# Softmax scores sent through DRAM and used an iteration later, in a 64-graph residual network kernel

One core of one Trainium2 chip. The metric is device time in microseconds (us), the median of several executions. The program runs on one core, so a run has one span and one granted TensorE clock; every run told here is of the fast state, with a granted clock of 0.995 to 0.999 (0.996 to 0.998 in the profiled runs).

## The reference

Two graph layers, each followed by a residual and a layer norm, over 64 graphs of 256 nodes with 512 features, in float32.

```python
def _L0(x, adj, W):
    deg = jnp.sum(adj, axis=-1, keepdims=True)
    agg = jnp.einsum('bij,bjf->bif', adj, x) / jnp.maximum(deg, EPS)
    return jax.nn.relu(jnp.einsum('bnf,of->bno', jnp.concatenate([x, agg], axis=2), W))

def _L1(X, adj, mask, Wqk, Wv):
    q, k = jnp.split(X @ Wqk, 2, axis=-1)
    v = X @ Wv
    agg = jnp.einsum('bij,bjd->bid', adj, k * mask[:, :, None])
    w = inv_scale * mask * jnp.einsum('bid,bid->bi', q, agg)     # one score a node
    return jax.nn.softmax(w, axis=1)[:, :, None] * v             # over the graph's 256 nodes

x = _layernorm(x + _L0(x, adj, W))
x = _layernorm(x + _L1(x, adj, nodemask, Wqk, Wv))
```

## The kernel before

One loop goes over the graphs as a software pipeline: iteration i runs layer 0 of graph i, layer 1's products of graph i-2, and the softmax and last stage (`finish`) of an older one. All products are cut into 2x2 blocks and multiplied in a seven-product scheme, so TensorE adds into one open accumulator `u` again and again, and between two such products ScalarE must copy `u` out. Layer 0's first part:

```python
def layer0_a(g):
    ...
    product(u, s["A11"], w["B11"])
    began = nc.scalar.copy(own[:, 0, :], u)
    product(p5, s["S1"], w["T1"])
    product(u, s["S2"], w["T2"], start=False)
    nc.scalar.copy(y[:, 0, :], u)
    product(p2, s["A12"], w["B21"])
    nc.vector.tensor_add(own[:, 0, :], p2, own[:, 0, :])
    product(u, s["S3"], w["T3"], start=False)
    nc.scalar.copy(y[:, 1, :], u)              # must end before the next product into u
    ...
def layer0_b(g):
    product(u, s["A22"], w["T4"], start=False) # "t,xT" in the profile
```

The scores of a graph lie one to a partition, but the softmax runs over the nodes. The kernel turns the scores of two graphs at a time into rows by TensorE and the probabilities back:

```python
def softmax_rows(k):                           # two graphs, every other iteration
    ...
    for t in range(NT):
        nc.tensor.transpose(wr[:, t, :], w[:, t, :], ident)
    nc.vector.reduce_max(top, wr.rearrange("g t p -> g (t p)"), axis=AX.X)
    ...
    nc.scalar.activation(e, wr, AF.Exp, bias=top, accum_out=total)
    ...
def softmax_cols(k, e):
    for t in range(NT):
        nc.tensor.transpose(ps[:, t, :], e[:, t, :], ident[:G, :G])
    nc.vector.tensor_copy(probs[k], ps)
```

A scheduler puts each engine's instructions in order from the program's text. `with tc.issue_after(ins):` holds what is written in its block behind `ins`, on the engine of `ins` alone; it sets an order and adds no wait.

Of the kernel before, what the change touches and what calls it, by code (L numbers as in the profile page):

```python
# [31 lines left out]
F32 = mybir.dt.float32  # L35
AF = mybir.ActivationFunctionType
# [2 lines left out]

P = 128  # L40
Q = 32
G = 2
DEG_EPS = 1e-6
LN_EPS = 1e-5

# [2 lines left out]
def resnorm_kernel(  # L48
# [21 lines left out]
    const = ctx.enter_context(tc.tile_pool(name="const", bufs=1))  # L70
    pool = ctx.enter_context(tc.tile_pool(name="pool", bufs=2))
    small = ctx.enter_context(tc.tile_pool(name="small", bufs=4))
    ps_mm = ctx.enter_context(tc.tile_pool(name="ps_mm", bufs=7, space=bass.MemoryType.PSUM))
    ps_tp = ctx.enter_context(tc.tile_pool(name="ps_tp", bufs=1, space=bass.MemoryType.PSUM))

    (xs, adjs, rows, xTs, sums0, sumsA, rdegs, vals, owns, x1s, x1Ts, sums1, aggs, vs, scores, probs,
     open0) = ({} for _ in range(17))

    def first(out, in_):

# [20 lines left out]
    with setup as sp:  # L101
        wqk = sp.tile([P, 2 * NA, F], F32, name="wqk")
        for a in range(NA):
            src = wqk_t.rearrange("(h a p) f -> a p h f", p=P, h=2)[a]
            first(wqk.rearrange("p (h a) f -> a p h f", h=2)[a], src)
        w0_of = w_t.rearrange("(k h p) o -> k p h o", p=P, h=H)
        for k in (0, 2):
            first(w0[:, k * H:(k + 1) * H, :], w0_of[k])
        load_t(0, first)
        for k in (3, 1):  # L110
            first(w0[:, k * H:(k + 1) * H, :], w0_of[k])
        load(0, first)
        mask_sb = const.tile([P, NT, B], F32, name="mask_sb")
        first(mask_sb, mask_t)
        load_t(1, first)
        load(1, first)
        loaded = first(w1[:, NF:, :], wv.rearrange("(c p) o -> p c o", p=P))

        ident = const.tile([P, P], F32, name="ident")
        make_identity(nc, ident)  # L120
        eps = const.tile([P, 1], F32, name="eps")
        nc.vector.memset(eps, LN_EPS)

        ps = [ps_mm.tile([P, F], F32, name="mm") for _ in range(NF)]
        for a in range(NA):
            for c in range(NF):
                nc.tensor.matmul(ps[c], wqk[:, a, c * P:(c + 1) * P], wqk[:, NA + a, :],  # L127
                                 start=(a == 0), stop=(a == NA - 1))
        for c in range(NF):
            nc.scalar.copy(w1[:, c, :], ps[c])  # L130
# [28 lines left out]
    def bank():  # L159
        return ps_mm.tile([P, F], F32, name="mm")  # L160
# [44 lines left out]
    def layer0_a(g):  # L205
        s, w = sums0[g], W0
        own = owns[g] = pool.tile([P, NT, F], F32, name="own")
        y = values(g)[:, 0]
        u, p5, p2 = bank(), bank(), bank()
# [3 lines that stand above are left out]
        product(u, s["S2"], w["T2"], start=False)  # L213
        nc.scalar.copy(y[:, 0, :], u)
        product(p2, s["A12"], w["B21"])
        nc.vector.tensor_add(own[:, 0, :], p2, own[:, 0, :])
        product(u, s["S3"], w["T3"], start=False)
        nc.scalar.copy(y[:, 1, :], u)  # L218
        nc.vector.tensor_add(y[:, 1, :], p5, y[:, 1, :])
        open0[g] = u, p5  # L220
        return began

    def layer0_b(g):
        s, w, own, y = sums0.pop(g), W0, owns[g], values(g)[:, 0]
# [12 lines left out]
    def gather_a(g):  # L237
# [7 lines left out]
        nc.vector.tensor_sub(t1, b12, b11)  # L245
        nc.vector.tensor_sub(t2, b22, t1)
        nc.vector.tensor_sub(t3, b22, b12)
        nc.vector.tensor_sub(t4, b21, t2)
        w = {"B11": b11, "B21": b21, "B22": b22, "T1": t1, "T2": t2, "T3": t3, "T4": t4}
        zr = aggs[g] = pool.tile([P, 2, NT, F], F32, name="zr")  # L250
        r11, r12, r21, r22 = (zr[:, k0:k1, t, h * HF:(h + 1) * HF] for t in range(NT) for h in range(2))
# [9 lines left out]
        def steps():  # L261
# [17 lines left out]
            twice(p5, "S4", "B22", start=False)  # L279
            nc.vector.tensor_add(r12, of(p5), r12)  # L280
            yield
        return steps()

    def combine0(g):
        own, z, rdeg, xg = owns[g], aggs[g][:, 0], rdegs.pop(g), xs.pop(g)
# [4 lines left out]
                                           op0=OP.max, op1=OP.add)  # L290

    def norm0(g):
        x1s[g] = pool.tile([P, NT, F], F32, name="x1", bufs=G + 4)
        layer_norm(owns.pop(g), x1s[g])
        for t in range(NT):
            nc.scalar.activation(values(g + 1)[:, 1, t, :], x1s[g][:, t, :], AF.Copy,  # L296
                                 scale=mask_sb[:, t, g:g + 1])
        x1Ts[g] = pool.tile([P, NF, N], F32, name="x1T")
        transpose_rows(x1s[g], x1Ts[g])
# [2 lines left out]
        sums1[g] = row_sums(x1Ts.pop(g), nc.vector)  # L302

    def layer1_steps(g):
        if g % G == 0:
            scores[g // G] = (small.tile([P, NT, G], F32, name="scores", bufs=2),
                              small.tile([P, G], F32, name="part", bufs=2))
        sc, part = scores[g // G]
        at = g % G
        s, w, agg = sums1.pop(g), W1, aggs.pop(g + 1)[:, 1]  # L310
        v = vs[g] = late.tile([P, NT, F], F32, name="v", bufs=G + 2)
        q = pool.tile([P, F], F32, name="q")

        def dot(a, t, to):
            nc.vector.scalar_tensor_tensor(q, a, 1.0, agg[:, t, :], op0=OP.mult, op1=OP.mult, accum_out=to)  # L315

        u = bank()
        product(u, s["A11"], w["B11"])
        nc.scalar.copy(q, u)
        dot(q, 0, part[:, at:at + 1])  # L320
        yield
        p5 = bank()
        product(p5, s["S1"], w["T1"])
        yield
        product(u, s["S2"], w["T2"], start=False)
        nc.scalar.copy(v[:, 0, :], u)  # L326
        yield
        p2 = bank()
        product(p2, s["A12"], w["B21"])
        dot(p2, 0, sc[:, 0, at:at + 1])  # L330
        yield
        product(u, s["S3"], w["T3"], start=False)
        nc.scalar.copy(v[:, 1, :], u)  # L333
        nc.vector.tensor_add(v[:, 1, :], p5, v[:, 1, :])  # L334
        yield
        product(u, s["A22"], w["T4"], start=False)
        dot(u, 1, sc[:, 1, at:at + 1])
        yield
        product(p5, s["S4"], w["B22"], start=False)
        nc.vector.tensor_add(v[:, 0, :], p5, v[:, 0, :])  # L340
        yield

    def softmax_rows(k):
        w, part = scores.pop(k)
        nc.vector.tensor_add(w[:, 0, :], w[:, 0, :], part)
        nc.vector.scalar_tensor_tensor(w, w, inv_scale, mask_sb[:, :, k * G:(k + 1) * G],
                                       op0=OP.mult, op1=OP.mult)
        wr = ps_tp.tile([G, NT, P], F32, name="tp")
        for t in range(NT):
            nc.tensor.transpose(wr[:, t, :], w[:, t, :], ident)  # L350
        top = small.tile([G, 1], F32, name="top")
        nc.vector.reduce_max(top, wr.rearrange("g t p -> g (t p)"), axis=AX.X)
        nc.vector.tensor_scalar(top, top, -1.0, None, op0=OP.mult)
        e = small.tile([G, NT, P], F32, name="e", bufs=2)
        total = small.tile([G, 1], F32, name="total")
        nc.scalar.activation(e, wr, AF.Exp, bias=top, accum_out=total)
        nc.vector.reciprocal(total, total)
        nc.vector.tensor_scalar(e, e, total, None, op0=OP.mult)
        return e

    def softmax_cols(k, e):
        ps = ps_tp.tile([P, NT, G], F32, name="tp")
        for t in range(NT):
            nc.tensor.transpose(ps[:, t, :], e[:, t, :], ident[:G, :G])  # L364
        probs[k] = small.tile([P, NT, G], F32, name="probs", bufs=2)
        nc.vector.tensor_copy(probs[k], ps)

    def finish(g):
        x1, v, p = x1s.pop(g), vs.pop(g), probs[g // G]
        o = pool.tile([P, NT, F], F32, name="o")  # L370
        for t in range(NT):
            nc.vector.scalar_tensor_tensor(o[:, t, :], v[:, t, :], p[:, t, g % G:g % G + 1], x1[:, t, :],  # L372
                                           op0=OP.mult, op1=OP.add)
        layer_norm(o, o)
        nc.sync.dma_start(out[g].rearrange("(t p) f -> p t f", p=P), o)
# [3 lines left out]
    def step(gen, n=1):  # L379
        for _ in range(n):  # L380
            next(gen, None)

    for i in range(B + G + 2):
        new = i < B
        if i + 2 < B:
            with tc.issue_after(loaded.ins):
                loaded = load(i + 2)
        if i == 1:
            W1 = weight_sums(w1, "t1_")
        k, at = divmod(i - G - 2, G)  # L390
        e = None
        if new:
            began = layer0_a(i)
        if at == 0 and 0 <= k < B // G:
            e = softmax_rows(k)
        if 0 <= i - 2 < B:
            turn(i - 2)
        l1 = layer1_steps(i - 2) if 0 <= i - 2 < B else iter(())
        step(l1)
        if new:  # L400
            layer0_b(i)
        if e is not None:
            softmax_cols(k, e)
        if 0 <= i - 2 - G < B:
            finish(i - 2 - G)
        z = gather_a(i) if i <= B else iter(())
        step(l1, 2)
        step(z)
        step(l1)
        step(z)  # L410
        step(l1)
        step(z)
        step(l1)
        step(z)
        step(l1)
        step(z)
        if new:
            combine0(i)
            norm0(i)
        if i + 1 < B:  # L420
            with tc.issue_after(began.ins):
                prepare(i + 1)


# [24 lines left out]
```

## Time and profile before

| | before |
|---|---|
| median of three runs | 1999.58 us (1999.43 to 1999.61) |
| span of the profiled run | 1996.4 us |
| busy: TensorE, VectorE, ScalarE | 99%, 76%, 31% |
| an iteration with / without softmax transposes | 30.78 / 30.16 us |
| 59 iterations, from the start of i = 4 (120.49) to that of i = 63 (1918.55) | 1798.06 us |

A profile names an instruction by engine, source line and operation, with its output and inputs (`mm<-t,xT` is the product of the weights `t` with `xT` into an accumulator bank). PE is TensorE, DVE VectorE, ACT ScalarE, POOL GpSimd, and SPq the SP queue, in which SyncE issues the DMAs. A line of a timeline has the start and the duration in us, the engine, source line, operation, output and inputs, and in brackets the idle time before it and what ended it. Line numbers move by four between the kernels: L156 and L218 here are L160 and L222 after. A line of the waits has the waiter and the awaited: us in total, times, longest. `PEld` is TensorE's weight load.

### The profile page before, as it was taken

To read this page: it belongs to the slowest core of one execution; us is meant where nothing else is said; L and a number is where in the kernel's file an instruction comes from. 1 tells how busy PE (TensorE), PEld (TensorE's weight loads), DVE (VectorE), ACT (ScalarE), POOL (GpSimd) and SP (SyncE) were. 2 spreads that over 40 slices of the span, in tenths; PEclk is the share of its full clock that TensorE was granted. 3 is DMA by queue.
4 is the path that set the end of the run, shared out by engine and by line. 5 is a ranking of instruction groups with operands and counts; after the bars stand their busy time and mean duration, and the time that the engine had idled before them with its cause. 6 is when DMAs were issued, how large, how long until landed. Compare 5 with 4: busy or idle time off the path is not lost.

```text
span 1996.4 us, 19070 instructions
## 1 busy us (share of the span) xinstructions
PE 1968.4 (99%) x5536; PEld 1029.0 (52%) x5536; DVE 1514.0 (76%) x3056; ACT 628.1 (31%) x1417; POOL 411.1 (21%) x518
## 2 busy tenths in 40 slices
PE   8999999999999999999999999999999999999996
PEld 3555555555555555555555555555555555555552
DVE  5667778777787777787777877777877778777776
ACT  2323333233233233332332332333323323323321
POOL 3122122221221121222212212212222121122100
PEclk9999999999999999999999999999999999999998
DMA  6333332332333333323333333333233233333211
GB/s 222 85 79 77 97 90 73 91 93 79 92 75 94 92 77 97 90 74 91 92 81 91 75 95 93 75 96 90 75 90 93 80 91 76 95 94 74 74 43 53
DMA packets 384902, 174.38 MB, mean 87 GB/s; under 512 B 283808, under 2 KB 349472, under 8 KB 384800
## 3 DMA queue, kind: packets, MB, share of 16 engines
q1 hardware_dynamic: 384800, 173.17, 32.9%
q8 instruction: 46, 0.75, 0.2%
q14 instruction: 56, 0.46, 0.1%
HBM read 105.97 MB, written 33.55 MB: 70 GB/s over the span
## 4 chain that ended last, share of the span: by engine, by line
PE 96%; DVE 2%; SPq 1%; DMA 0%; ACT 0%; issue 0%; DVEq 0%; ACTq 0%
PE mm L156 76%; PE mm L255 19%; SPq L171 1%; PE mm L127 1%; PE tp L364 0%; PE tp L350 0%; DVE st L178 0%; DMA xT<-x_t 0%; DMA wqk<-wqk_t 0%; DVE own L289 0%; DVE own L287 0%; DVE o L372 0%; ACT vals L296 0%; DVE x L184 0%; DMA x1T<-sq 0%
## 5 line engine op out<-in xcount | busy, mean ns | idle before, releaser
L156 PE MATMUL mm<-w,s 128*128 128x512 f32 x1024 | 481.2, 592 | 0.0
L156 PE MATMUL mm<-t,s 128*128 128x512 f32 x1024 | 463.9, 595 | 0.0
L156 PEld LDWEIGHTS mm<-t,s 128*128 128x128 f32 x1024 | 192.1, 190 | 229.2 <-issue 213.6
L156 PEld LDWEIGHTS mm<-w,s 128*128 128x128 f32 x1024 | 194.6, 190 | 191.1 <-issue 162.6
L156 PE MATMUL mm<-w,x1T 128*128 128x512 f32 x512 | 240.8, 593 | 2.3 <-DMA x1T<-sq 2.3
L156 PE MATMUL mm<-w,xT 128*128 128x512 f32 x512 | 240.9, 592 | 0.0
L197 POOL TENSOR_TENSOR sa<-adj 128x128 f32<-128x128 f32 x64 | 45.8, 716 | 780.0 <-PE mm L255 778.5
L148 POOL TENSOR_TENSOR s<-xT 128x256 f32<-128x256 f32 x64 | 46.7, 730 | 704.5 <-PE mm L156 685.4
L255 PE MATMUL mm<-tv,sa 128*128 128x256 f32 x768 | 187.5, 379 | 0.4 <-DVE tv L245 0.4
L255 PEld LDWEIGHTS mm<-tv,sa 128*128 128x128 f32 x768 | 145.8, 190 | 76.1 <-issue 60.1
L229 DVE TENSOR_TENSOR vals<-mm,vals 128x512 f32<-128x512 f32 x64 | 44.3, 692 | 134.6 <-PE mm L156 134.6
L156 PEld LDWEIGHTS mm<-w,xT 128*128 128x128 f32 x512 | 97.3, 190 | 94.6 <-issue 91.3
L334 DVE TENSOR_TENSOR v<-mm,v 128x512 f32<-128x512 f32 x64 | 44.3, 692 | 130.9 <-ACT v L333 130.9
L287 DVE SCALAR_TENSOR_TENSOR own<-zr,rdeg,own 128x512 f32<-128x512 f32 x128 | 107.6, 841 | 42.4 <-ACT zr L277 42.3
L156 PEld LDWEIGHTS mm<-w,x1T 128*128 128x128 f32 x512 | 94.8, 190 | 83.7 <-issue 79.4
L315 DVE SCALAR_TENSOR_TENSOR q<-mm,zr 128x512 f32<-128x512 f32 x128 | 88.1, 688 | 65.6 <-PE mm L156 65.6
L326 ACT COPY v<-mm 128x512 f32<-128x512 f32 x64 | 37.4, 585 | 298.1 <-PE mm L156 298.1
L156 PE MATMUL mm<-t,x1T 128*128 128x512 f32 x256 | 125.5, 612 | 0.9 <-ACT v L333 0.7
L255 PE MATMUL mm<-vals,adj 128*128 128x256 f32 x512 | 121.6, 380 | 2.3 <-DVE vals L229 1.9
L156 PE MATMUL mm<-t,xT 128*128 128x512 f32 x256 | 120.6, 593 | 2.8 <-ACT vals L218 2.8
L255 PEld LDWEIGHTS mm<-vals,adj 128*128 128x128 f32 x512 | 97.0, 190 | 44.6 <-issue 25.1
L372 DVE SCALAR_TENSOR_TENSOR o<-v,probs,x 128x512 f32<-128x512 f32 x128 | 118.4, 963 | 0.0
(81 smaller groups left out, 2588.2 us busy)
## 6 DMA issues: line engine op xcount, KB each, us to landing
xT<-x_t SPq DMA_DIRECT2D x64, 512.0 KB, 4.3
x<-x SPq DMA_DIRECT2D x64, 512.0 KB, 3.6
x1T<-sq SPq DMA_DIRECT2D x1024, 32.0 KB, 2.0
out<-o SPq DMA_DIRECT2D x64, 512.0 KB, 4.0
adj<-adj_t SPq DMA_DIRECT2D x64, 256.0 KB, 2.7
rows<-adj SPq DMA_DIRECT2D x64, 256.0 KB, 4.5
wqk<-wqk_t SPq DMA_DIRECT2D x4, 512.0 KB, 5.1
w<-w_t SPq DMA_DIRECT2D x4, 512.0 KB, 8.8
```

The costliest lines, as they stand in the source:

```text
L127: nc.tensor.matmul(ps[c], wqk[:, a, c * P:(c + 1) * P], wqk[:, NA + a, :], start=(a == 0), stop=(a == NA - 1))
L148: eng.tensor_add(s1, a21, a22)
L156: nc.tensor.matmul(ps, a[:, c, :], b[:, c, :], start=start and c == 0, stop=(c == H - 1), skip_group_check=True)
L171: nc.sync.dma_start(to[b * Q:(b + 1) * Q, :, a, :], sq[a * Q:(a + 1) * Q, b].rearrange("p c t q -> p (c t) q"))
L197: nc.gpsimd.tensor_add(sa[:, 0], a21, a22)
L229: nc.vector.tensor_add(y[:, 0, :], p5, y[:, 0, :])
L255: nc.tensor.matmul(ps[:, k * HF:(k + 1) * HF], sumsA[g - k][a], w[b][:, n, :], start=start and n == 0, stop=True, skip_group_check=True)
L287: nc.vector.scalar_tensor_tensor(own[:, t, :], z[:, t, :], rdeg[:, t:t + 1], own[:, t, :], op0=OP.mult, op1=OP.add)
L315: nc.vector.scalar_tensor_tensor(q, a, 1.0, agg[:, t, :], op0=OP.mult, op1=OP.mult, accum_out=to)
L326: nc.scalar.copy(v[:, 0, :], u)
L334: nc.vector.tensor_add(v[:, 1, :], p5, v[:, 1, :])
L372: nc.vector.scalar_tensor_tensor(o[:, t, :], v[:, t, :], p[:, t, g % G:g % G + 1], x1[:, t, :], op0=OP.mult, op1=OP.add)
```

## The change

The intent is to take the transposes off the engine that is 99% busy. The scores are turned in 32x32 blocks by VectorE, written to a DRAM scratch as one row of 256, and read back to all 128 partitions at once. Each partition then computes the same maximum and sum from the row, and its own two probabilities from its own column; nothing has to be turned back. The row is used an iteration after it is read. The last two graphs keep TensorE's transposes. The last stage is held behind the aggregation's four subtractions, and softmax and the next graph's preparation behind the `own` addition.

```diff
-G = 2
+LAG = 4                                      # also sets how many buffers v and x1 have
-    ps_mm = ... bufs=7 ... ; ps_tp = ... bufs=1 ...
+    ps_mm = ... bufs=8 ... ; dram = ctx.enter_context(tc.tile_pool(name="dram", bufs=2, space=bass.MemoryType.DRAM))
-        nc.vector.tensor_add(own[:, 0, :], p2, own[:, 0, :])
+        added = nc.vector.tensor_add(own[:, 0, :], p2, own[:, 0, :])
-        nc.vector.tensor_sub(t4, b21, t2)
+        summed = nc.vector.tensor_sub(t4, b21, t2)
+    def write_scores(g):
+        w = columns[g] = wide[g % 2]
+        scale_scores(g, w[:, :NT])
+        turned = small.tile([P, Q], F32, name="turned", bufs=2)
+        nc.vector.transpose(turned, w)
+        d = rows_d[g] = dram.tile([NT, P], F32, name="d")
+        for a in range(P // Q):
+            nc.sync.dma_start(d[:, a * Q:(a + 1) * Q], turned[a * Q:a * Q + NT, :])
+    def read_scores(g):
+        row = rowsW[g] = small.tile([P, N], F32, name="row", bufs=2)
+        nc.sync.dma_start(row, rows_d.pop(g).rearrange("t p -> (t p)").partition_broadcast(P))
+    def softmax(g):
+        nc.vector.reduce_max(top, row, axis=AX.X, negate=True)
+        nc.scalar.activation(row, row, AF.Exp, bias=top, accum_out=total)
+        nc.scalar.activation(p, w[:, :NT], AF.Exp, bias=top)
+        nc.vector.reciprocal(total, total)
+        nc.vector.tensor_scalar(p, p, total, None, op0=OP.mult)
     for i in range(...):
+        if 0 <= i - 3 < B - 2:
+            write_scores(i - 3)
+            read_scores(i - 3)
         ...                                  # softmax_rows, softmax_cols and finish taken out
+        if 0 <= i - LAG < B - 2:
+            with tc.issue_after(began.ins), tc.issue_after(added.ins):
+                softmax(i - LAG)
+            with tc.issue_after(summed.ins):
+                finish(i - LAG)
-            with tc.issue_after(began.ins):
+            with tc.issue_after(began.ins), tc.issue_after(added.ins):
                 prepare(i + 1)
... (cut: declarations, the kept transposed softmax of the last two graphs)
```

## The prediction

> **What bounds the kernel now.** I read the page from the top: busy shares, then TensorE's idle time by cause, then the timeline of one pair of iterations, then the tail.
>
> ```profile
> span 1996.4 us, 19070 instructions
> PE 1968.4 (99%) x5536; PEld 1029.0 (52%) x5536; DVE 1514.0 (76%) x3056; ACT 628.1 (31%) x1417; POOL 411.1 (21%) x518
> PE 96%; DVE 2%; SPq 1%; DMA 0%; ACT 0%; issue 0%; DVEq 0%; ACTq 0%
> L350 PE MATMUL tp<-ident,scores 128*2 128x128 f32 x64 | 12.2, 273 | 0.0
> L364 PE MATMUL tp<-ident,e 2*128 2x2 f32 x64 | 9.0, 207 | 2.4 <-DVE e L358 2.4
> ```
>
> TensorE is busy 99% and is 96% of the chain that ended last. Its named waits add up to about 16 us, all in the first 80 us or the last 40. So in the 60 middle iterations only two things can move the time: matmul work taken away, and a new wait of TensorE. VectorE's 76% and ScalarE's 31% matter only through such a wait. The last two rows are the 128 softmax transposes.
>
> Their true price is read from TensorE's timeline, since busy spans overlap.
>
> ```profile
> 912.72 1.88 PE L156 MATMUL mm<-w,xT 128*128 128x512 f32 x4
> ...
> 921.30 0.38 PE L350 MATMUL tp<-ident,scores 128*2 128x128 f32 x2
> 921.52 1.88 PE L156 MATMUL mm<-w,x1T 128*128 128x512 f32 x4
> ...
> 924.96 1.88 PE L156 MATMUL mm<-w,s 128*128 128x512 f32 x4
> 926.77 0.28 PE L364 MATMUL tp<-ident,e 2*128 2x2 f32 x2
> 926.98 3.70 PE L156 MATMUL mm<-t,s 128*128 128x512 f32 x8
> ...
> 943.50 1.88 PE L156 MATMUL mm<-w,xT 128*128 128x512 f32 x4
> ```
>
> This iteration runs from 912.72 to 943.50: 30.78 us. The next one, with no transposes, ends at 973.66: 30.16 us. The four transposes and the gaps around them cost 0.62 us a pair: 0.22 for the first two, and about 0.4 for the second two, whose short streams leave small gaps on both sides. The 30.16 is matmul time almost alone: 14 products of four matmuls at 0.429 us and 28 half-width matmuls at 0.215 make 30.0.
>
> **What the Trainium skill says.** "TensorE: Matmul & The Clock Gate", section "Step-by-step: what each phase is for", says that weight loads are pulled ahead while matmuls stay in program order. The trace agrees: loads sit under the previous matmul, and a matmul that waits loses this overlap too, measured below. "DMA: Bandwidth & Descriptors", section "Anatomy of one DMA — SWDGE (gpsimd) path", puts some 2.0 us of fixed cost on a transfer, mostly its write receipt. It describes another issuing path, but the 16 x1T pieces of 32 KB land in a median of 2.0 us here, so I use 2 us for each hop. "Trainium Architecture — The Big Picture", section "Inside one NeuronCore", gives each engine its own instruction stream, joined to others only by semaphores: an instruction put ahead of another on ScalarE delays it though the data are unrelated. My main cost term rests on that.
>
> **The change, part by part.** (a) *Transposes leave TensorE* for graphs 0 to 61. Thirty pairs lie in steady iterations: 30 x 0.62 = 18.6 us saved. The 31st pair lay in the tail, where TensorE waits for a DMA anyway; I give it 0.3.
>
> (b) *The DRAM round trip.* VectorE's scaled scores are ready about 27.8 us into an iteration (971.15 + 0.16 - 943.50). Four tiny writes, 2 us, one row read, 2 us: the row is there some 6 us later. The built order shows it used by the maximum only a whole iteration after that, so some 28 us of slack. On the SP queue the read makes the queue wait about 2 us for the writes, just after an adjacency load and before an x load that itself waits until 3.76 us into the next iteration (947.26 - 943.50); the x1T pieces start at about 8.3 us. I see no delay from it. Traffic added is 128 KB a graph, at 33% DMA use.
>
> (c) *VectorE and ScalarE.* VectorE loses about 1.5 us a pair and gains about 1.2 us a graph (a 128x256 maximum, estimated at 0.40 from the 0.411 us of the 2x256 one, and small instructions). Free on a 76% engine, unless in a chain.
>
> (d) *The last stage behind the subtractions.* The `o` work goes as one block behind the four `tv` subtractions, ending about 18.7 us in (961.16 + 1.10 - 943.50 = 18.76). `o` twice 0.7, statistics 1.3, the `zr` addition 0.7 and the aggregates bring ScalarE's root to 22.3-22.8; its `zr` copy behind that ends at about 23.4, while TensorE wants it at 24.06 (967.56). It fits by 0.5 us. No gain either, as TensorE didn't wait there before.
>
> (e) *A new wait, the costly part.* The built order on ScalarE is: two masked `vals` copies, the wide exponential over `row`, then the copy `vals<-mm` that must drain the accumulator before TensorE's product `t_4,xT`. Before, the exponential followed that copy. The exponential needs the maximum, which on VectorE comes behind the `sq` transposes and the `own` addition. An iteration that starts at 973.66 in the kernel before has this layout already:
>
> ```profile
> 973.66 1.88 PE L156 MATMUL mm<-w,xT 128*128 128x512 f32 x4
> 980.65 1.30 DVE L167 STREAM_TRANSPOSE sq<-x 128x512 f32<-128x512 f32 x2
> 981.87 0.65 DVE L216 TENSOR_TENSOR own<-mm,own 128x512 f32<-128x512 f32 x1
> 982.44 0.58 ACT L218 COPY vals<-mm 128x512 f32<-128x512 f32 x1 [0.80 <-PE mm L156]
> 984.18 1.45 PE L156 MATMUL mm<-t,xT 128*128 128x512 f32 x3
> ```
>
> `own` starts 8.21 us in. An independent instruction follows it 0.58 us later (953.02 - 952.45 = 0.57 elsewhere): maximum from 8.79 to 9.19. Semaphore to ScalarE 0.05-0.09: exponential from 9.25, its slot about 0.45 (0.41 for the 128x256 `rows` activation, 0.46 for the old exponential). Copy from 9.70, 0.585 long: ends at 10.29. TensorE's slot is 984.18 - 973.66 - 0.22 = 10.30. That seems just in time, but a wait costs more than its end, as the start-up shows:
>
> ```profile
> 69.77 0.56 ACT L218 COPY vals<-mm 128x512 f32<-128x512 f32 x1
> 70.38 1.98 PE L156 MATMUL mm<-t,xT 128*128 128x512 f32 x4 [0.51 <-ACT vals L218]
> 72.20 1.88 PE L156 MATMUL mm<-w,s 128*128 128x512 f32 x4
> ```
>
> The copy ends at 70.33, the matmul starts 0.05 later, and its four take 1.82 instead of 1.72 because the weights were not loaded ahead. Loss = copy's end + 0.15 - slot = 10.29 + 0.15 - 10.30 = 0.14, say 0.15 us an iteration. The exponential is there in iterations 4 to 63: 60 x 0.15 = 9 us. A lag of TensorE moves all its followers alike, so it adds up.
>
> (f) *Tail.* Before, both last graphs' softmax and `o` stages follow the last product. That stretch ran from 1984.46 to 1992.04, 7.6 us for two graphs; one alone takes about 4.5 (`o` 1.4, statistics 1.2, aggregates 0.3, root 0.6, normalizing 1.0). Now only graph 63's is left there, 3.1 us less; but graphs 62 and 61 finish between the last products on the same engine, and a transpose and a q copy stall TensorE there for about a microsecond. By adding VectorE's durations in the built order I get about 1.1 us net.
>
> Sum: -18.6 - 0.3 + 9 - 1.1 = -11, from 1999.6 to about 1988.
>
> **The rivals.** *No stall*: the whole 20 us is kept, 1979.5. For it: if the maximum and exponential take 0.15 us less than I put, the copy is out of the way, and the margin in (e) is that thin. Against it: the arithmetic from measured durations says the copy ends exactly at the slot. *A deeper stall*: if the wide maximum or exponential costs 0.2 us more, the loss is 0.35 an iteration, 21 us, and the kernel stands at 2000. For it: both work on SBUF over 128 partitions, and I have only similar instructions. *A second stall from (d)*: the root that waits for VectorE's aggregates sits ahead of two ScalarE copies that TensorE needs; 0.5 us later and it adds up to 0.3 an iteration, 18 us. Against it: 0.5 us of slack, and GpSimd's sums, beside which VectorE's instructions are longer, end at 18.2. *The DRAM round trip shows*: only if the writes landed 28 us late; near nothing.
>
> **Range and chances.** The stall term from 0 to 0.3 us spans 1979 to 1997, so the range is 1979 to 1997 with 1988 in it. Two per cent faster means 1959.6, which no term can give: 20 us is all there is. Two per cent slower means 2039.6, a stall of a whole microsecond in each iteration: 3 in 100, for a scheduler order I have misread.
>
> **What would show it.** The tp groups shrink from 128 matmuls to 8. TensorE's waits gain a row for the product `t_4,xT` on ScalarE's second `vals` copy, some 60 times, with under 0.1 us of idle each and the rest as a longer first matmul, and the iteration is 30.16 + 0.15 = 30.3 us. If that row is missing and the iteration is 30.15, (e) was wrong and the time is near 1979. If the row names a `zr` or `v` copy, it was (d). If TensorE waits on a DMA in the middle, (b) was wrong.

## More of the kernel before

```profile
PEld mm L156 <- ACT vals L218: 5.3, 3, 2.5
PE mm L156 <- ACT vals L218: 2.8, 3, 1.6
```

ScalarE's second `vals` copy delays TensorE three times in this kernel, all during start-up.

## The result, and the profile after

| | before | after |
|---|---|---|
| median, same rounds | 1999.51 us (1998.76 to 1999.61, 4 runs) | 1989.21 us (1988.24 to 1989.65, 4 runs) |
| ratio of fast runs, 95% interval | | 0.9949 (0.9931 to 0.9966) |
| span of the profiled run | 1996.4 us | 1986.5 us |
| iteration | 30.78 / 30.16 us | 30.30 us |

A ratio here and below is the mean time of one kernel's fast runs over that of the other's in the same rounds, so it isn't quite the ratio of the medians beside it. The change is a gain of half a per cent, within the 2% that counts as the same.

The page of the kernel after, the lines that answer to the first ones shown in the prediction:

```profile
span 1986.5 us, 19676 instructions
PE 1960.3 (99%) x5416; PEld 1017.5 (51%) x5416; DVE 1566.5 (79%) x3218; ACT 650.0 (33%) x1543; POOL 419.6 (21%) x518
PE 96%; DVE 1%; SPq 1%; DMA 0%; ACT 0%; issue 0%; DVEq 0%
```

TensorE has 120 matmuls less (5536 to 5416) and bounds the kernel as before. VectorE and ScalarE have more to do, which by itself costs nothing. The three waits that matter, from the list of waits of the kernel after:

```profile
ACT row L367 <- DVE top L365: 73.9, 60, 1.2
PEld mm L160 <- ACT vals L222: 47.2, 63, 2.5
PE mm L160 <- ACT vals L222: 2.8, 3, 1.6
```

The second row is the new one: it was 5.3 us, 3 times, and is 47.2 us, 63 times, the 3 of the start-up and 60 more. The third row hasn't moved, and a reader who looks only for TensorE's matmuls in the waits finds nothing. The list shows no idle time of the matmul in the middle; its weights come late. How that costs time shows in the timeline of one iteration, which starts at 908.87:

```profile
908.87 1.88 PE L160 MATMUL mm<-w,xT 128*128 128x512 f32 x4
...
917.08 0.65 DVE L220 TENSOR_TENSOR own<-mm,own 128x512 f32<-128x512 f32 x1
917.65 0.40 DVE L365 TENSOR_REDUCE top<-row 128x1 f32<-128x256 f32 x1
918.09 0.51 ACT L367 ACTIVATE row<-row,top 128x256 f32<-128x256 f32 x1 [1.23 <-DVE top L365]
918.59 0.56 ACT L222 COPY vals<-mm 128x512 f32<-128x512 f32 x1
919.21 1.98 PE L160 MATMUL mm<-t,xT 128*128 128x512 f32 x4
921.03 1.88 PE L160 MATMUL mm<-w,s 128*128 128x512 f32 x4
...
939.17 1.88 PE L160 MATMUL mm<-w,xT 128*128 128x512 f32 x4
```

The copy ends at 919.15. TensorE's product starts at 919.21, only 0.04 us behind its slot (917.45 + 1.72 = 919.17), but the next one starts 1.82 us later instead of 1.72: together 0.14 us, in every one of these iterations. The page counts TensorE as busy all the while.

Where the 9.9 us of the two profiled spans come from, by landmarks of TensorE's timeline: up to the start of i = 4, 120.49 before and 121.06 after (+0.57); from there to the start of i = 63, 1798.06 before and 1787.71 after (-10.35); from there to the end, 77.85 before and 77.73 after (-0.12). Only the middle is a sharp measure. Over the eleven kernels profiled here the start ran from 120.48 to 122.13 us and the end from 75.3 to 78.7, without following the edits, so a microsecond in either can't be put down to an edit by one profile each.

### The profile page after: what moved, and what is told of

It is laid out like the page before. It is cut to its first block, busy times and chain, and to the rows that moved or that the text cites. A ratio compares the mean times of both kernels' runs of the same rounds, so it can differ in the third digit from the quotient of the medians.

```text
span 1986.5 us, 19676 instructions
## 1 busy us (share of the span) xinstructions
PE 1960.3 (99%) x5416; PEld 1017.5 (51%) x5416; DVE 1566.5 (79%) x3218; ACT 650.0 (33%) x1543; POOL 419.6 (21%) x518
## 4 chain that ended last, share of the span: by engine, by line
PE 96%; DVE 1%; SPq 1%; DMA 0%; ACT 0%; issue 0%; DVEq 0%
PE mm L160 76%; PE mm L259 19%; SPq L175 1%; PE mm L131 1%; DVE st L182 0%; DMA adj<-adj_t 0%; DMA wqk<-wqk_t 0%; DVE own L293 0%; DVE own L291 0%; DMA x1T<-sq 0%; DVE x L188 0%; DVE o L396 0%; ACT vals L300 0%; DVE v L341 0%; DVE t L141 0%
## 5 line engine op out<-in xcount | busy, mean ns | idle before, releaser
L185 ACT ACTIVATE rstd<-mv,eps 128x2 f32<-128x2 f32 x128 | 37.9, 296 | 341.3 <-DVE mv L183 341.3
L160 PE MATMUL mm<-t,xT 128*128 128x512 f32 x256 | 126.8, 617 | 2.8 <-ACT vals L222 2.8
L215 ACT COPY own<-mm 128x512 f32<-128x512 f32 x64 | 37.5, 586 | 227.4 <-PE mm L160 227.4
```

Source lines behind the costliest of these rows:

```text
L160: nc.tensor.matmul(ps, a[:, c, :], b[:, c, :], start=start and c == 0, stop=(c == H - 1), skip_group_check=True)
L185: nc.scalar.activation(rstd, mv[:, :, 1], AF.Ln, bias=eps)
```

## Experiments

Three theories. **T**: the change saves TensorE 0.62 us a pair of graphs (about 18.9 us), and gives 0.14 us an iteration back (59 x 0.14 = 8.3 us) since ScalarE's exponential now stands ahead of the copy that TensorE waits for. **R1**: the missing half went to the DRAM round trip and its place in the SP queue. **R2**: it went to the held last stage, whose root stands on ScalarE ahead of two copies that TensorE needs. "Middle" is the stretch of 59 iterations above. All kernels gave right results.

| run | median us | ratio to before, 95% interval | iteration us | middle us |
|---|---|---|---|---|
| before | 1999.51 | 1 | 30.78 / 30.16 | 1798.06 |
| after | 1989.21 | 0.9949 (0.9931 to 0.9966) | 30.30 | 1787.71 |
| e1_exp_behind_copy | 1979.89 | 0.9898 (0.9885 to 0.9912) | 30.16 | 1779.20 |
| e2_max_not_held | 1979.73 | 0.9897 (0.9884 to 0.9911) | 30.16 | 1779.20 |
| e3_exp_longer | 2000.67 | 1.0001 (0.9987 to 1.0014) | 30.52 | 1800.48 |
| e6_transposes_back | 1997.88 | 0.9987 (0.9974 to 0.9999) | 30.79 / 30.15 | 1798.05 |
| e4_finish_not_held | 1988.80 | 0.9942 (0.9930 to 0.9955) | 30.30 | 1787.58 |
| e5_prepare_not_held | 1986.86 | 0.9933 (0.9920 to 0.9945) | 30.30 | 1787.58 |
| e7_lag3 | 1987.63 | 0.9934 (0.9920 to 0.9947) | 30.30 | 1787.67 |
| e8_swap | 1974.31 | 0.9870 (0.9857 to 0.9884) | 30.08 | 1774.52 |
| e9_swap_prepare | 1975.38 | 0.9871 (0.9854 to 0.9887) | 30.08 | 1774.52 |

e1, e2, e3 and e6 ran on one chip, with the kernel before at 1999.6 (1998.94 to 2002.68); e4, e5, e7 and e8 on another turn, before at 1999.19; e9 alone, before at 2001.36.

### The exponential behind the copy

```diff
-        nc.scalar.copy(y[:, 1, :], u)
+        drained = nc.scalar.copy(y[:, 1, :], u)
... (cut: `layer0_a` returns `drained` as well)
-            with tc.issue_after(began.ins), tc.issue_after(added.ins):
+            with tc.issue_after(drained.ins), tc.issue_after(added.ins):
                 softmax(i - LAG)
```

> Theory T (ScalarE's wide exponential stands ahead of the copy that TensorE's product t_4,xT waits for, 0.14 us an iteration): with the exponential queued behind that copy the iteration falls from 30.30 to 30.16 us, 60 x 0.14 = 8.4 us, so about 1981 us and no more late weight load on that copy in the middle. Rival R1 (the rest of the expected 20 us went to the DRAM round trip and its place in the SP queue) and rival R2 (it went to the last stage, whose root now stands ahead of two copies): this edit touches neither, so 1989, within 1.5 us.

Measured: 1979.89 us, iteration 30.16. Its timeline at the same place:

```profile
914.76 1.88 PE L160 MATMUL mm<-w,x1T 128*128 128x512 f32 x4
914.96 0.59 ACT L222 COPY vals<-mm 128x512 f32<-128x512 f32 x1 [0.80 <-PE mm L160]
914.97 0.40 DVE L365 TENSOR_REDUCE top<-row 128x1 f32<-128x256 f32 x1
915.45 0.51 ACT L367 ACTIVATE row<-row,top 128x256 f32<-128x256 f32 x1
916.48 1.88 PE L160 MATMUL mm<-t,xT 128*128 128x512 f32 x4
918.20 1.02 PE L160 MATMUL mm<-w,s 128*128 128x512 f32 x2
```

The copy starts as soon as its product is done and ends at 915.55, and the product is in its slot (916.48, the next 1.72 us later). In this iteration the instructions are those of the kernel after, and TensorE's order is the same; what differs is ScalarE's order, and on VectorE one `vals` addition that comes one place earlier. T holds, and R1 and R2, which this edit doesn't touch, can explain none of these 8.5 us of the middle.

### The maximum not held

```diff
-            with tc.issue_after(began.ins), tc.issue_after(added.ins):
+            with tc.issue_after(began.ins):
                 softmax(i - LAG)
```

> The hold of the maximum behind the own addition is taken away; the built order then has the maximum an iteration's part earlier and the exponential ahead of the row sums, where ScalarE idled 2.2 us. Theory T: the copy is free, 30.16 us an iteration, about 1981 us, the same as with the exponential behind the copy. R1 and R2: 1989. If holding the maximum was what made the change gain at all, it would be slower than 1989.

Measured: 1979.73 us, the same middle to the hundredth. In an iteration that starts at 905.68 the exponential now stands more than six microseconds ahead of the copy, and the product is in its slot (914.26 + 1.72):

```profile
908.08 0.51 ACT L367 ACTIVATE row<-row,top 128x256 f32<-128x256 f32 x1
914.47 0.59 ACT L222 COPY vals<-mm 128x512 f32<-128x512 f32 x1 [0.80 <-PE mm L160]
915.98 1.88 PE L160 MATMUL mm<-t,xT 128*128 128x512 f32 x4
```

Two quite different places for the exponential, one later and one earlier, both free the copy. The hold behind the `own` addition, which the change added, is what put the exponential into the one tight place.

### A longer exponential

```diff
-        nc.scalar.activation(row, row, AF.Exp, bias=top, accum_out=total)
+        spare = small.tile([P, 2, N], F32, name="spare", bufs=1)
+        nc.scalar.activation(spare, row.unsqueeze(1).broadcast_to([P, 2, N]), AF.Exp, bias=top, accum_out=total)
-        nc.vector.tensor_scalar(p, p, total, None, op0=OP.mult)
+        nc.vector.tensor_scalar(p, p, total, 2.0, op0=OP.mult, op1=OP.mult)
```

> The exponential runs over the row twice (512 instead of 256 elements, the sum halved afterwards; a right result), about 0.27 us longer by the 0.41 us of a 256-element and 0.67 us of a 512-element activation on SBUF. Theory T: every bit of it lands on TensorE, 60 x 0.27 = 16 us, about 2005 us. R1 and R2: ScalarE is 33% busy, so 1989.

Measured: 2000.67 us, iteration 30.52. The timeline:

```profile
924.13 0.72 ACT L368 ACTIVATE spare<-row,top 128x512 f32<-128x512 f32 x1 [1.23 <-DVE top L365]
924.86 0.56 ACT L222 COPY vals<-mm 128x512 f32<-128x512 f32 x1
...
925.47 1.98 PE L160 MATMUL mm<-t,xT 128*128 128x512 f32 x4
927.29 1.02 PE L160 MATMUL mm<-w,s 128*128 128x512 f32 x2
```

The exponential is 0.21 us longer (median 0.721 against 0.508), less than the 0.27 I expected, and the iteration is 0.22 us longer (1800.48 - 1787.71 = 12.77 over 59). ScalarE's time at this place goes into the kernel's one to one, on an engine that is 33% busy in the kernel after. An exponential longer by 0.21 us loses the whole gain of the change.

### The transposes put back

The kernel e1, and in even iterations from 4 on, before `turn` and before the last-stage code, four transposes of constants that nobody reads:

```diff
+        back = i % 2 == 0 and 4 <= i < B
+        if back:
+            b = bank()
+            for t in range(NT):
+                tc.keep_in_program_order(nc.tensor.transpose(b[:2, t * P:(t + 1) * P], ident[:, :2], ident))
...
+        if back:
+            b = bank()
+            for t in range(NT):
+                tc.keep_in_program_order(nc.tensor.transpose(b[:, t * 2:(t + 1) * 2], ident[:2, :], ident[:2, :2]))
```

> As the run with the exponential behind the copy, and with four transposes of constants put back on TensorE in the 30 even iterations, at the places where the kernel before had them; nobody reads them. If the transposes were worth 0.62 us a pair: 30 x 0.62 = 18.6 us over the run without them, about 1999.6, which is the kernel before. If the change's gain came from elsewhere (fewer VectorE waits, the eighth bank), the transposes cost only their busy time, some 0.66 us less overlap, and the time stays clearly under 1995.

Measured: 1997.88 us, 18.0 above e1 on the same chip; the middle is 1798.05 us, against 1798.06 in the kernel before. So the four transposes a pair and the exponential's place account for the whole difference of the middle, and nothing in it is left for the eighth bank, the shorter list of VectorE waits and the DRAM traffic, with which this kernel still runs. The 1.7 us by which its median is below the kernel before's on that chip (1999.6) lie outside the middle.

### The last stage not held

```diff
-            with tc.issue_after(summed.ins):
-                finish(i - LAG)
+            finish(i - LAG)
```

> The last stage is not held behind the aggregation's subtractions. By the durations of the trace the subtractions then end some 1.6 us later, and still 6 us before TensorE needs the last of them. Theory T: no effect, 1989 within 1.5 us, iteration 30.30. Rival R2 (the held stage costs, its root stands ahead of two copies): faster, towards 1981. A third view, that the hold is what makes the change pay: slower by more than 2 us, with TensorE waiting on a tv subtraction or a vals addition.

Measured: 1988.80 us, iteration 30.30. The hold of the last stage is worth nothing in either direction: without it the last subtraction ends 19.7 us into the iteration instead of 18.9, and TensorE wants its result at 26.9 (935.73 less 908.87 in the kernel after). R2 is out. The subtractions end less than the expected 1.6 us later: two of the four now run after GpSimd's sums have ended (926.25) and take 0.68 us each, where those beside the sums take 1.21.

### The preparation not held

```diff
-            with tc.issue_after(began.ins), tc.issue_after(added.ins):
+            with tc.issue_after(began.ins):
                 prepare(i + 1)
```

> The next graph's preparation is held behind ScalarE's first copy alone, as in the kernel before. The middle should not move (30.30). TensorE reached the fifth iteration 0.57 us later than in the kernel before (121.06 against 120.49 us); if this hold did that, it is back at about 120.5 and the time at 1988.6; if not, 1989.2.

Measured: 1986.86 us (1985.69 to 1988.88); the middle doesn't move, and i = 4 starts at 120.61. That fits the first half of the expectation. But e9 below has the same edit and starts i = 4 at 121.25, so this start can't be put down to the hold: of the kernels that keep it, e1 and e2 start at 122.13 and 121.63, e7 and e8 at 120.48 and 120.59. The landmark includes the wait for the first weights (`wqk`), which varied from 4.4 to 5.7 us between profiles. Inconclusive: that the hold costs anything isn't shown.

### The row used at once

```diff
-LAG = 4
+LAG = 3
-    for i in range(B + LAG - 1):
+    for i in range(B + 3):
```

> The row is used in the iteration in which it is read, not one later. The read is issued about 1.0 us into the iteration; with some 2 us to land it is there at 3.5 to 4 us, and the maximum runs at 8.8. Theory T: no effect on the middle, 30.30 us, 1989 within 1.5 us. Rival R1 (the round trip is what costs): the maximum waits for a DMA and the time is 2 us or more above 1989.

Measured: 1987.63 us, iteration 30.30. The read is issued 0.83 us into the iteration, and the maximum still runs at 8.8 us with no wait for a DMA ahead of it. (`LAG` also sets the buffers of `v` and `x1`, which fall by one each; in the iteration compared, the order of instructions on every engine is that of the kernel after.) The round trip is hidden even without the extra iteration, and the deferral that the change is named after wasn't needed for the time. That the writes and the read cost nothing in the SP queue either is shown by e1 and e6, which keep both and have the kernel before's 30.16 us without transposes and 30.79 with them. With that, R1 is out for the middle.

### A swap in layer 1

The last regular loss in e1 is some 0.08 us at the product `t,x1T`, whose accumulator is copied out only 0.08 us before its slot: in e1 it starts at 931.10 and the next one at 932.89, and the lines below show the same loss in the kernel after. The edit is e1 with two steps of `layer1_steps` exchanged:

```diff
+        product(u, s["S3"], w["T3"], start=False)
+        nc.scalar.copy(v[:, 1, :], u)
+        nc.vector.tensor_add(v[:, 1, :], p5, v[:, 1, :])
+        yield
         p2 = bank()
         product(p2, s["A12"], w["B21"])
         dot(p2, 0, sc[:, 0:1])
-        yield
-        product(u, s["S3"], w["T3"], start=False)
-        nc.scalar.copy(v[:, 1, :], u)
-        nc.vector.tensor_add(v[:, 1, :], p5, v[:, 1, :])
         yield
```

> As the run with the exponential behind the copy, and in layer 1 the product w,x1T with its dot comes after the product that fills the second v half instead of ahead of it, so that the copy of v has a longer product to hide under. The matmul t_4,x1T loses about 0.085 us an iteration now, with its weights loaded late (0.06 us of waiting, 1.80 instead of 1.72 us). If that is right: 62 x 0.085 = 5.3 us under the run without the swap, about 1975.5, iteration 30.07. If another copy becomes late instead: as without it, 1981, or above.

Measured: 1974.31 us, iteration 30.08. TensorE in the kernel after, then in e8:

```profile
933.07 1.03 PE L259 MATMUL mm<-tv,sa 128*128 128x256 f32 x4
933.93 1.96 PE L160 MATMUL mm<-t,x1T 128*128 128x512 f32 x4
935.73 1.03 PE L259 MATMUL mm<-tv,adj 128*128 128x256 f32 x4
```

```profile
926.64 1.03 PE L259 MATMUL mm<-tv,sa 128*128 128x256 f32 x4
927.50 1.88 PE L160 MATMUL mm<-t,x1T 128*128 128x512 f32 x4
929.22 1.03 PE L259 MATMUL mm<-tv,adj 128*128 128x256 f32 x4
```

The product takes 1.80 us to the next one's start in the first and 1.72 in the second. With a further 4.7 us off the middle this is the fastest version, 1.3% under the kernel before, and with 30.08 us an iteration it is close to the 30.04 us of matmul alone (14 x 4 x 0.429 + 28 x 0.215).

### All helpful edits together

e8 and the preparation not held.

> The three helpful edits together: exponential behind the copy, the swap in layer 1, and the preparation not held behind the own addition. The last was worth 2 us alone, at the start and the end and not in the middle. If the three are independent: 1974.3 - 2 = 1972 us, iteration 30.07 us. If freeing the preparation disturbs the new order of layer 1, 1974 or more.

Measured: 1975.38 us, ratio 0.9871 against 0.9870 for e8: the same within the intervals, and the same middle. The 2 us of e5 didn't come back. The expectation of 1972 was wrong, and the reading of e5 as a gain isn't borne out.

## Why the prediction was right

**The transposes' price (a).** Thirty pairs at 0.62 us were put at 18.6. The middle of e6 less that of e1 is 18.85 us over 30 pairs, 0.63 each. Reading the price from the timeline of two neighbouring iterations, and not from the busy column (21.2 us for 128 transposes with overlaps), gave it. VectorE's extra work (c) was put too low: its busy time grew by 52.5 us, where the figures in (c) make 28. It cost nothing by itself, as e1 has the 30.16 us of an iteration without transposes in the kernel before.

**The new wait (e).** Measured from the iteration's start, predicted and found: the maximum 8.79 to 9.19 and 8.78 to 9.18; the exponential from 9.25 and 9.22; the copy from 9.70 and 9.72, its end 10.29 and 10.28; the loss 0.14 and 0.14. Part of this is luck in two sizes that cancel: I put the exponential's slot at 0.45 us, and it is 0.50, while the copy took 0.56 instead of 0.585 and the exponential began 0.03 earlier. The kernel stood on the steep side: e3 shows that 0.21 us more costs 12.8 us, e1 that the copy out of the way saves 8.5. The forecast of "60 times" holds in the count. That an instruction put ahead of another on ScalarE delays it though the data are unrelated, on which the cost term rested, is what e3 and e1 show: 0.21 us more ahead of the copy costs an iteration 0.22 us, and none ahead of it saves 0.14. What I said the waits would show was wrong in form: the idle time appears at the weight load, and none of it at the matmul.

**The round trip (b) and the held last stage (d)** were forecast to cost and bring nothing, and e7 and e4 agree. Of the 2 us put for each hop the profile after shows only the queue's wait for the writes, 88.8 us in all or 1.4 a graph; it gives no landing time for the row. The root on ScalarE came at 22.2 to 22.7 us (931.07 to 931.59, less 908.87) where I had 22.3 to 22.8, its `zr` copy ended at 23.3 where I had 23.4.

**The ends, (a)'s last term and (f).** Here the sum missed. I expected 1.4 us less at the end (0.3 and 1.1), and the stretch from i = 63 on is 0.12 us shorter. The pieces of it: iteration 63 takes 30.15 us in both; from the first matmul on graph 63's `x1T` to the end, 28.20 us before (1968.20 to 1996.4) and 26.95 after (1959.55 to 1986.5), 1.25 less, as the step said. But that matmul starts 20.63 us after the beginning of iteration 64 (1959.55 - 1938.92) instead of 19.50 (1968.20 - 1948.70), since the SP queue had issued the last x1T piece only 18.37 us in (1957.29) instead of 17.05 (1965.75). One of them held the SP queue for 1.80 us where the others take 0.61; why, the profile doesn't say. It isn't a mark of the change: one piece in the kernel before took 1.72 us, and the last sixteen took 10.4 us in e3, e6, e8 and e9 as in the kernel before, and 10.6 to 11.6 in the others. The start is 0.57 us longer where I had nothing, which is within what the start varied between kernels. So the ends brought 0.45 us more instead of 1.4 less, and the middle 10.35 less instead of 9.6. The second error makes good 0.75 of the first's 1.85 us: by luck, the sum missed by 1.1 us only (-9.9 instead of -11).

**The rivals.** "No stall" (1979.5) is what e1 and e2 are, 1979.9 and 1979.7. "A deeper stall" (2000) is what e3 is. The thin margin was seen rightly, and so was its worth.

## What to carry to other kernels

On a kernel bound by one engine at 99%, look for what other engines' queues put ahead of the instruction that releases it: here work on an engine that is 33% busy cost its full length where it stood (e3), and moving it a place later was free (e1). Work out that instruction's end from the rows of the same iteration before building on a saving, and count a late release as more than the lateness, since the weights come late too. When a change names several ideas, undo each: here one carried all the gain, two nothing, and a hold added with them took half of it back.

## What the Trainium skill lacked or had wrong

- "TensorE: Matmul & The Clock Gate", section "Step-by-step: what each phase is for", tells that weight loads are pulled ahead, and gives no price for when that fails. Here a product whose accumulator is drained too late costs about the copy's end plus 0.15 us less its slot: 0.14 us although the product starts 0.04 us late (four matmuls in 1.82 instead of 1.72 us), shown in the list of waits only at the weight load.
- "VectorE: DVE Perf Modes", section on the TRN2 errata, has 224 cycles plus one an element for ScalarE from SBUF at 1.2 GHz. For 256 elements that is, as an estimate, 0.400 us, which the row sums with an accumulated output show (0.412). The exponential with a bias for each partition took 0.508 for 256 elements and 0.721 for 512, where the table makes an estimated 0.613 for the latter: some 0.11 us more, which the table doesn't have. The runs point to the operand and not to the function: in the kernel after, an exponential of 128x2 took 0.204 us without a bias and 0.294 with one, and a plain copy of 128x512 scaled by a per-partition operand took 0.714. This is a gap of that table and not of the skill, since the page "ScalarE: Activation LUTs" prices such an operand apart.
- No page that I used prices small float32 transposes inside a stream of matmuls. Two of 128x2 and two of 2x128, with the gaps around them, cost 0.63 us (18.85 us over 30 groups of four).
